# Additive attention scores: 16 tanh terms on three engines, or three groups of them as ratios of two matmuls

## The chip, the cores and the metric

The kernel runs on one core of one Trainium2 chip. TensorE (PE) multiplies matrices into PSUM, ScalarE (ACT) evaluates functions, VectorE (DVE) and GpSimd (POOL) work elementwise, SyncE (SP) and the queues of the other engines issue DMAs. The metric is the device time of one execution in microseconds (us). Before the change it was 9234.1 us, the median of 3 runs (9233.7 to 9238.85).

## The reference

The input x is (4, 32, 128, 128) in float32. Layer 0 (spectral convolutions with attention over 32 images) is not changed and is left out here. Layer 1 sees each of the 4 batch items as 4096 tokens of 128 channels:

```
h = layer norm of t
f = h @ W1[:128]                      # 16 numbers per token, as a query
g = h @ W1[128:]                      # 16 numbers per token, as a key
scores[i, j] = sum over a of w2[a] * tanh(f[i, a] + g[j, a] + b1[a])  + b2
e = exp(scores), for keys j before query i only (strictly)
t = t + (e @ h) / (sum of e + 1e-10)
t = t + two best of eight experts on layer norm of t, weighted by a softmax router
```

So for each pair of a query and an earlier key 16 tanh values are weighted and summed; that is some 33 million pairs.

## The kernel before, in words

`layer0` (L67 to L510) runs first and writes x1 to DRAM. Of it only a few rows are spoken of below: image norms with squares on ACT (L236), copies from PSUM by ACT and DVE in turn (L216, L218), the mix of modes with matmuls of 32 rows on different quadrants of the partitions (L453) and their products on DVE (L454), products and sums on POOL (L377, L489, L505), and powers on POOL (L64).

`layer1` (L513 to L804) goes through 16 chunks, 4 of each batch item, of IC = 1024 queries. Keys and queries are the same tokens, so a chunk also adds 8 blocks of 128 keys. In one chunk:

- `prepare` (called by `begin`) loads the tokens xc, norms them on DVE and POOL (`layer_norm`, L567 to L578, with the square at L572), transposes them on PE (L586), and makes the keys' numbers gk.
- `queries` makes, for each of the 16 hidden units, a tile f with the query's number on every partition (matmul L616, copy on DVE L623).
- For each block jb of 128 keys up to the diagonal there is one score tile of 128 keys by up to 1024 queries (only the columns from lo on). Each of the 16 units costs one tanh on ACT (L740), with the key's number as bias. For 5 units (A_PE) PE multiplies by w2 on a diagonal and sums in PSUM (L745). For the other 11, DVE multiplies and adds (L750, L754), and PE adds the sum through an identity matrix (L763). Then comes Exp (L765), and on the diagonal a mask by POOL (L767).
- After every four key blocks (JG) PE makes the attention's output po from e and the normed keys (L786), and DVE adds it to att (L796, L798).
- `finish` of the chunk before is written between two such groups: division by the sum (L635), addition to xc on POOL (L636), norm, transposes, router logits (L652), the two best experts in small DVE operations (L654 to L687), and then for each of 8 token blocks and both halves of the experts a matmul with 128 rows (L693), one with 1 row for the bias (L696), and four DVE operations that add the weighted result to xc (L698). The store follows. `begin` of the next chunk is written at the end of a chunk.

The order of the instructions on each engine is set by a scheduler of the tile framework from the program's order and the buffers of the pools. Each tag of a pool has its own buffers: 2 in PSUM for each of sc, m and o, 4 for th, 5 for e, 17 for f. An instruction waits on its own engine's queue, in order, until its operands are there and its buffer is free.

Of the kernel before, what the change touches and what calls it, by code (L numbers as in the profile page):

```python
# [7 lines left out]
F32 = mybir.dt.float32  # L8
# [5 lines left out]
P = 128  # L14
B, T, H, C = 4, 32, 128, 128  # x; an image of layer 0 is H x C, a block of layer 1 has H tokens
NH = 32  # heads of layer 0
KX, KY = 64, 33  # modes kept of a 128 x 128 image: rows 0..31, -32..-1; columns 0..32
KA = 17  # columns of the K, Q and V weights' modes (their rows: 0..15, -16..-1)
GI = 8  # images at a time
NPIX = H * C  # L20
A = 16  # width of layer 1's additive attention
A_PE = 5  # terms of its scores that the tensor engine sums; the vector engine sums the others
NE = 8  # experts
IC = 1024  # queries at a time
NB = IC // P
JG = 4  # key blocks for each accumulation of the attention's output

# places in the packed row of small parameters
# [5 lines left out]
def _constants():  # L34
    """Transforms and masks, from shapes alone."""
# [22 lines left out]

def _inv_std(nc, small, out, var, eps, nhalf):
    """out = (var + eps) ** -0.5"""  # L60
    n = out.shape[1]
    ve = small.tile([P, n], F32, name="ve", tag=f"ve{n}")
    nc.vector.tensor_scalar(ve, var, eps, None, ALU.add)  # L63
    nc.gpsimd.tensor_tensor(out, ve, nhalf.to_broadcast([P, n]), ALU.pow)  # L64


def layer0(tc, x, kcw, qcw, vcw, pcw, m0cw, m1cw, heads, small_row, by_p, inv_cols, x1):  # L67
# [9 lines left out]
    # (re | im) of a row transform of a real image, of i times it, and of minus it  # L77
# [20 lines left out]
    # score weights by mode, for the modes' real and imaginary parts  # L98
# [3 lines left out]
    # value weights: on partition 32g + head, columns ky = 4k + g  # L102
# [8 lines left out]
    with tc.tile_pool(name="l0_prep", bufs=1) as prep:  # L111

        def padded(src, name):
# [3 lines left out]
            for ri in range(2):  # L117
# [4 lines left out]
                # column 0 of a real image's spectrum is Hermitian  # L122
# [16 lines left out]
        # W = q conj(k), scaled for the inner product of two 64 x 64 images  # L139
# [27 lines left out]
        # row -32 of column 0 is its own mirror in a 64 x 64 image, and so real  # L167
# [11 lines left out]
        # G = P (v skip + V) + (P skip) V  # L179
# [32 lines left out]
    def evacuate(out, in_):  # L212
        """PSUM to SBUF, by the scalar and the vector engine in turn."""
        flip[0] ^= 1
        if flip[0]:
            nc.scalar.copy(out, in_)  # L216
        else:
            nc.vector.tensor_copy(out, in_)  # L218

    def image_means(src):  # L220
        """Means over each image of src [w, images, c], on every partition, in PSUM."""
        n = src.shape[1]
        s = small.tile([P, n], F32, name="s", tag=f"s{n}")
        nc.vector.tensor_reduce(s, src, AX.X, ALU.add)  # L224
        m = ps.tile([P, n], F32, name="m", tag="stat")
        nc.tensor.matmul(m, mean_w, s, start=True, stop=True)  # L226
        return m

    def inorm(src, out, w=None, b=None):
        """Instance norm of src [w, images, c] into out."""  # L230
# [15 lines left out]
    def transform(images, mirrored=None):  # L246
        """Modes X and iX of GI images [w, c], in PSUM, on partitions (part, kx) by (image, ky);
        mirrored gets column 32 of their 64 x 64 part."""
# [23 lines left out]
    def inverse(spec, take):  # L272
        """Images [w, c] of GI half spectra [(part, kx), image, ky]: take(k, four) gets those of
        images k .. k + 3, in PSUM."""
# [16 lines left out]
    for b in range(B):  # L291
# [60 lines left out]
        # column 32 of a 64 x 64 image is its own mirror, and its row -32 real  # L352
# [160 lines left out]
def layer1(tc, x1, w1, expert_w, expert_b, router_w, small_row, out):  # L513
    nc = tc.nc
    nblk = T  # blocks of 128 tokens of one b
# [3 lines left out]
        tc.tile_pool(name="l1_f", bufs=17),  # L519
        tc.tile_pool(name="l1_work", bufs=2),  # L520
        tc.tile_pool(name="l1_small", bufs=3),
        tc.tile_pool(name="l1_ps", bufs=2, space=PSUM),
    ]
    const, keys, fpool, work, small, ps = (p.__enter__() for p in pools)

    ident = const.tile([P, P], F32, name="ident1")
# [5 lines left out]
    w1t = const.tile([P, 2, A], F32, name="w1t")  # L532
    nc.sync.dma_start(out=w1t, in_=w1.rearrange("(s h) a -> h s a", s=2))
# [8 lines left out]
    # w2[a] on the diagonal  # L542
    w2d = const.tile([P, A_PE, P], F32, name="w2d")
    for a in range(A_PE):
        nc.vector.tensor_scalar(w2d[:, a], ident, par[:, W2 + a : W2 + a + 1], None, ALU.mult)
    # keys before queries: 1 where the column (query) is greater than the row (key)
# [11 lines left out]
    # ranks that fall with the expert's index, for ties  # L558
# [3 lines left out]

    def layer_norm(src, dst):
        """Layer norm over c of src [token, blocks, c] into dst."""
# [15 lines left out]
    def transposed(src):  # L580
        """[c, tokens] of src [token, blocks, c]."""
        xt = work.tile([P, IC], F32, name="xt", tag="xt")
        for k in range(0, NB, 4):
            pt = ps.tile([P, 4, P], F32, name="pt", tag="m")
            for j in range(4):
                nc.tensor.transpose(pt[:, j], src[:, k + j, :], ident)  # L586
            nc.vector.tensor_copy(xt[:, k * P : (k + 4) * P], pt.rearrange("p j t -> p (j t)"))
        return xt

    def prepare(b, i0, kx, gk):  # L590
        """Queries i0 .. i0 + IC: their tokens, and what they are as keys."""
# [3 lines left out]
        xt = transposed(kx[:, i0 : i0 + NB, 0:C])  # L595
        pg = ps.tile([P, NB, A], F32, name="pg", tag="m")
        for k in range(NB):
            nc.tensor.matmul(
                pg[:, k], xt[:, k * P : (k + 1) * P], w1t[:, 1], start=True, stop=True
            )  # L600
        nc.vector.tensor_tensor(
            gk[:, i0 : i0 + NB],
            pg,
            par[:, B1 : B1 + A].unsqueeze(1).to_broadcast([P, NB, A]),
            ALU.add,
        )
        return xc, xt

    def queries(xt):
        """Each query's part of the scores' argument, on every partition."""  # L610
        fq = []
        for a in range(A):
            f = fpool.tile([P, IC], F32, name="f", tag="f")
            for h in range(0, IC, 512):
                pf = ps.tile([P, 512], F32, name="pf", tag="m")
                nc.tensor.matmul(  # L616
                    pf,
                    w1t[:, 0, a : a + 1].to_broadcast([P, P]),
                    xt[:, h : h + 512],
                    start=True,  # L620
                    stop=True,
                )
                nc.vector.tensor_copy(f[:, h : h + 512], pf)  # L623
            fq.append(f)

        return fq

    def finish(b, i0, xc, att):
        """Adds the attention and the experts' layer to tokens xc, and stores them."""
# [9 lines left out]
        x2 = work.tile(full, F32, name="x2", tag="x2", bufs=1)  # L639
        layer_norm(xc, x2)  # L640
        x2t = transposed(x2)
# [8 lines left out]
        pl = ps.tile(fe, F32, name="pl", tag="m")  # L650
# [39 lines left out]
        for k in range(NB):  # L690
            for e0 in range(0, NE, 4):
                px = ps.tile([P, 4, C], F32, name="px", tag="m")
                nc.tensor.matmul(  # L693
                    px, x2t[:, k * P : (k + 1) * P], we[:, e0 : e0 + 4], start=True, stop=False
                )
                nc.tensor.matmul(px, ones1, eb[:, e0 : e0 + 4], start=False, stop=True)  # L696
                for e in range(4):
                    nc.vector.scalar_tensor_tensor(  # L698
                        xc[:, k],
                        px[:, e],  # L700
# [7 lines left out]
    def begin(b, i0, last):  # L708
        """As prepare, with the keys' tiles of the chunk before in the same b."""
        if i0 == 0:  # L710
            # normed tokens with a column of ones, and each key's part of the scores' argument
            kx = keys.tile([P, nblk, C + 1], F32, name=f"kx_{b}", tag="kx")
            nc.gpsimd.memset(kx[:, :, C : C + 1], 1.0)
            gk = keys.tile([P, nblk, A], F32, name=f"gk_{b}", tag="gk")
        else:
            kx, gk = last
        return (kx, gk, *prepare(b, i0, kx, gk))

    pending = None
    chunks = [(b, i0) for b in range(B) for i0 in range(0, nblk, NB)]  # L720
    ready = None
    for n_chunk, (b, i0) in enumerate(chunks):
        if ready is None:
            ready = begin(b, i0, None)
        kx, gk, xc, xt = ready
        fq = queries(xt)
        att = work.tile([P, NB, C + 1], F32, name="att", tag="att")
        group = []
        for jb in range(i0 + NB):
            lo = max(0, jb - i0) * P  # L730
            cuts = [(max(lo, h), h + 512) for h in range(0, IC, 512) if lo < h + 512]
# [129 lines left out]
```

## Time and profile before

| what | us |
| --- | --- |
| median of 3 runs | 9234.1 |
| span of the profiled execution | 9233.0 |
| first DMA issue of layer 1 (load of par) | 3061.0 |
| first normed keys ready | 3083.2 |
| start of the last finish | 9143.5 |
| busy PE, DVE, ACT, POOL | 6954.0, 6341.1, 5327.9, 625.2 |
| mean granted clock of PE | 0.795 of full |

The span runs from the first to the last instruction of the profiled execution. Busy times are sums over the whole span; the slices of the page, 40 equal ones of 231 us, tell where they fall. In a group's line the number after the bar is the busy time in us, then the mean of one instruction in ns, then the idle time ahead of it and what ended it. "PEld" is the loading of the stationary matrix, which can lie beside a matmul. A float32 matmul on PE appears as two records.

### The profile page before, as it was taken

The page shows a single profiled execution, that of the slowest core. Times are in us where ns is not written, and L with a number is a line of the kernel's source. Part 1 is how long each engine was busy: PE and PEld are TensorE (multiplying, and loading weights), DVE is VectorE, ACT ScalarE, POOL GpSimd, SP SyncE. Part 2 cuts the span into 40 slices and gives each one's busy share as a digit, 9 for nine tenths or more (in the row PEclk, how much of TensorE's full clock was granted, in tenths as well). Part 3 has the DMA queues.
Part 4 walks back from the last instruction along what each step waited for, and adds up shares of the span by engine and source line. Part 5 has one row for each costly group of instructions (what it writes and reads, how often), then busy time and mean ns, then how long its engine had stood idle before and what let it go on. Part 6 is the DMA issues. An engine that isn't in the chain of part 4 may idle for free.

```text
span 9233.0 us, 58632 instructions
## 1 busy us (share of the span) xinstructions
PE 6954.0 (75%) x19444; PEld 3500.2 (38%) x19444; DVE 6341.1 (69%) x8087; ACT 5327.9 (58%) x5917; POOL 625.2 (7%) x444
## 2 busy tenths in 40 slices
PE   3854954764584688787788878788888878887877
PEld 2443343343343333333333333343333333334333
DVE  4834754564474677777777777777877777777775
ACT  1012011011101477979867888986887895879795
POOL 1011111101101000000000000000000001000000
PEclk8655655655655789898999898898989899989987
DMA  1000000000000000000000000000000000000000
GB/s 29 2 5 14 2 3 16 2 3 5 4 0 7 12 5 5 0 5 0 0 5 5 5 0 5 0 0 10 0 5 0 5 0 5 5 3 0 3 0 3
DMA packets 72207, 42.00 MB, mean 5 GB/s; under 512 B 2524, under 2 KB 71262, under 8 KB 71871
## 3 DMA queue, kind: packets, MB, share of 16 engines
q1 hardware_dynamic: 45341, 24.55, 1.0%
q10 hardware_dynamic: 26562, 13.71, 0.5%
q8 instruction: 153, 2.51, 0.1%
q14 instruction: 151, 1.24, 0.0%
HBM read 18.82 MB, written 16.78 MB: 4 GB/s over the span
## 4 chain that ended last, share of the span: by engine, by line
PE 35%; ACT 34%; issue 13%; DVE 12%; POOL 5%; DMA 0%; SPq 0%; POOLq 0%; ACTq 0%; DVEq 0%
ACT th L740 29%; PE sc L745 13%; PE px L693 3%; PE px L696 3%; ACT e L765 3%; DVE s L224 2%; POOL r L64 2%; PE po L786 2%; PE sc L763 2%; PE pz L258 2%; DVE acc L754 2%; PE four L288 2%; PE sc L381 1%; DVE f L623 1%; PE pf L616 1%
## 5 line engine op out<-in xcount | busy, mean ns | idle before, releaser
L740 ACT ACTIVATE th<-f,gk 128x1024 f32<-128x1024 f32 (+7 forms) x5120 | 4676.1, 992 | 1087.0 <-PE sc L745 395.1
L754 DVE SCALAR_TENSOR_TENSOR acc<-th,par,acc 128x1024 f32<-128x1024 f32 (+7 forms) x3200 | 3512.8, 1098 | 832.9 <-ACT th L740 670.9
L745 PE MATMUL sc<-th,w2d 128*128 128x512 f32 (+3 forms) x5760 | 2866.5, 645 | 469.7 <-ACT th L740 450.2
L745 PEld LDWEIGHTS sc<-th,w2d 128*128 128x128 f32 x5760 | 1168.1, 217 | 1986.0 <-issue 1015.2
L786 PE MATMUL po<-kx,e 128*128 128x129 f32 x4224 | 609.7, 292 | 413.1 <-ACT e L765 316.6
L786 PEld LDWEIGHTS po<-kx,e 128*128 128x128 f32 x4224 | 526.0, 197 | 697.6 <-ACT e L765 503.4
L616 PE MATMUL pf<-xt,w1t 128*128 128x512 f32 x1024 | 527.8, 634 | 117.4 <-DVE f L623 115.7
L226 PE MATMUL m<-s,mean_w 128*128 128x8 f32 x384 | 112.5, 366 | 633.9 <-DVE s L224 626.5
L216 ACT COPY v<-pv 128x264 f32<-128x264 f32 x48 | 18.4, 384 | 986.7 <-PE pv L278 986.7
L698 DVE SCALAR_TENSOR_TENSOR xc<-px,wgt,xc 128x128 f32<-128x128 f32 x1024 | 340.4, 348 | 248.0 <-PE px L696 235.2
L763 PE MATMUL sc<-acc,ident 128*128 128x512 f32 (+3 forms) x1152 | 508.5, 559 | 0.0
L767 POOL TENSOR_TENSOR e<-e,later 128x128 f32<-128x128 f32 x128 | 88.5, 692 | 5313.5 <-ACT e L765 5313.5
L453 PE MATMUL mp<-pr,g_im 32*128 32x512 f32 x528 | 408.2, 1039 | 0.0
L453 PE MATMUL mp<-pr,g_re 32*128 32x512 f32 x528 | 403.9, 1067 | 2.9 <-DVE mix L454 2.9
L623 DVE COPY f<-pf 128x512 f32<-128x512 f32 x512 | 338.9, 684 | 51.9 <-PE pf L616 50.2
L226 PEld LDWEIGHTS m<-s,mean_w 128*128 128x128 f32 x384 | 96.5, 312 | 664.7 <-DVE s L224 418.6
L64 POOL TENSOR_TENSOR r<-ve,nhalf 128x8 f32<-128x8 f32 x128 | 210.1, 1641 | 2037.3 <-DVE ve L63 1967.3
L765 ACT ACTIVATE e<-sc,par 128x1024 f32<-128x1024 f32 (+3 forms) x320 | 306.3, 957 | 58.0 <-PE sc L763 52.0
L750 DVE TENSOR_SCALAR acc<-th,par 128x1024 f32<-128x1024 f32 (+3 forms) x320 | 210.8, 659 | 177.8 <-ACT th L740 177.8
L693 PE MATMUL px<-we,xt 128*128 128x512 f32 x512 | 331.8, 735 | 0.0
L616 PEld LDWEIGHTS pf<-xt,w1t 128*128 128x128 f32 x1024 | 174.5, 194 | 392.9 <-DVE f L623 338.8
L460 DVE TENSOR_REDUCE yf<-mix 128x16 f32<-128x1024 f32 x264 | 322.4, 1221 | 0.3
(230 smaller groups left out, 5777.8 us busy)
## 6 DMA issues: line engine op xcount, KB each, us to landing
x<-x SPq DMA_DIRECT2D x16, 512.0 KB, 3.2
xc<-x SPq DMA_DIRECT2D x16, 512.0 KB, 4.0
out<-xc ACTq DMA_DIRECT2D x16, 512.0 KB, 3.2
x<-in_x SPq DMA_DIRECT2D x8, 512.0 KB, 8.4
x<-in_x ACTq DMA_DIRECT2D x8, 512.0 KB, 9.2
pr<-pr SPq DMA_DIRECT2D x8, 128.0 KB, 2.9
pw<-in_pcw SPq DMA_DIRECT2D x1, 528.0 KB, 5.2
pr<-pr ACTq DMA_DIRECT2D x4, 128.0 KB, 2.3
```

The lines of the kernel that those rows point to most:

```text
L64: nc.gpsimd.tensor_tensor(out, ve, nhalf.to_broadcast([P, n]), ALU.pow)
L453: nc.tensor.matmul(mp, gw[pq, k, :], pr[pq, th], start=True, stop=True)
L616: nc.tensor.matmul(pf, w1t[:, 0, a : a + 1].to_broadcast([P, P]), xt[:, h : h + 512], start=True, stop=True,)
L623: nc.vector.tensor_copy(f[:, h : h + 512], pf)
L693: nc.tensor.matmul(px, x2t[:, k * P : (k + 1) * P], we[:, e0 : e0 + 4], start=True, stop=False)
L698: nc.vector.scalar_tensor_tensor(xc[:, k], px[:, e], wgt[:, k, e0 + e : e0 + e + 1], xc[:, k], ALU.mult, ALU.add,)
L740: nc.scalar.activation(th[:, lo:], fq[a][:, lo:], AF.Tanh, bias=gk[:, jb, a : a + 1])
L745: nc.tensor.matmul(sc[:, c0:c1], w2d[:, a], th[:, c0:c1], start=n_pe == 0, stop=False)
L754: nc.vector.scalar_tensor_tensor(acc[:, lo:], th[:, lo:], par[:, W2 + a : W2 + a + 1], acc[:, lo:], ALU.mult, ALU.add,)
L763: nc.tensor.matmul(sc[:, c0:c1], ident, acc[:, c0:c1], start=False, stop=True)
L765: nc.scalar.activation(e[:, lo:], sc[:, lo:], AF.Exp, bias=par[:, B2 : B2 + 1])
L786: nc.tensor.matmul(po[:, k - k0], t[:, k * P : (k + 1) * P], kx[:, j, :], start=j == js[0][0], stop=j == js[-1][0],)
```

## The change

The sum of w2[a] * tanh(u[a]) over a group of m units is written as a ratio. With tanh(u) = (e^u - e^-u) / (e^u + e^-u), the common denominator of m units is the product of the (e^u[a] + e^-u[a]), which is the sum over all 2^m choices of signs s of exp(sum of s[a] u[a]). The numerator is the same sum with each term multiplied by the sum of s[a] w2[a]. As u[a] is a key's part plus a query's part, each exponential is a key's factor times a query's factor, so both sums are inner products over the choices of signs, which are matmuls. Groups of 6, 5 and 5 units give 64, 32 and 32 choices, 128 rows in all.

- New inputs: the matrix of signs (17 x 128), W1 transposed, and a 17 x 2 array with b1, w2 and b2. At the start of layer 1 two matmuls make mq and mk (channels to sign choices) and a third kbias and kmul.
- `prepare` makes km = Exp(mk x + kbias), kc = km * kmul and qm = Exp(mq x). `queries` and the w2d diagonals are gone. km and kc are kept for all keys of a batch item.
- A chunk is done in two halves of QC = 512 queries. In each half `scores` is called for each key block: three matmuls D into three PSUM banks, Ln on ACT and Exp of its negative (1/D), three matmuls N, a product on DVE, two additions on POOL, Exp on ACT, and the mask on the diagonal on POOL.
- The attention's output is accumulated in PSUM over all key blocks of a half, and copied once to att.
- PSUM tags are now d (3 banks), n (3 banks) and o (2 banks), each with one buffer. The transposes, router logits and expert products use d and n as well: px takes the two in turn, one for each block of tokens.
- `finish` and `begin` are called behind key block 2 of the first and the second half.
- One table of functions that holds both Ln and Exp is loaded at the start of layer 1.

The core of the diff (comments that the change removes and the wiring of inputs are left out):

```diff
-IC = 1024  # queries at a time
+GROUP_SIZES = (6, 5, 5)
+DSCALE = 128.0
+IC = 1024
+QC = 512
+QB = QC // P
...
+def _signs():
+    s = np.zeros((A + 1, P), np.float32)
+    a = col = 0
+    for m in GROUP_SIZES:
+        for n in range(2**m):
+            for i in range(m):
+                s[a + i, col + n] = -1.0 if n >> i & 1 else 1.0
+        a, col = a + m, col + 2**m
+    s[A, : 2 ** GROUP_SIZES[0]] = 1.0
+    return s
...
-        tc.tile_pool(name="l1_ps", bufs=2, space=PSUM),
+        tc.tile_pool(name="l1_ps", bufs=1, space=PSUM),
...
+    tc.keep_in_program_order(nc.scalar.preload_act_table_set("natural_log_exp_and_others"))
...
+    def wide(name, tag):
+        return ps.tile([P, 3, 512], F32, name=name, tag=tag)
...
+        xt = transposed(kx[:, i0 : i0 + NB, 0:C], "d")
+        i = slice(i0 * P, i0 * P + IC)
+        for m, dst, bias, tag in ((mk, km[:, i], kbias, "n"), (mq, qm, 0.0, "d")):
+            pz = wide("pz", tag)
+            for h in range(2):
+                nc.tensor.matmul(
+                    pz[:, h], m, xt[:, h * 512 : (h + 1) * 512], start=True, stop=True
+                )
+            nc.scalar.activation(
+                dst.rearrange("p (h t) -> p h t", h=2), pz[:, :2], AF.Exp, bias=bias
+            )
+        nc.vector.tensor_scalar(kc[:, i], km[:, i], kmul, None, ALU.mult)
...
         for k in range(NB):
+            px = wide("px", "dn"[k % 2])
             for e0 in range(0, NE, 4):
-                px = ps.tile([P, 4, C], F32, name="px", tag="m")
+                pe = px[:, e0 // 4].rearrange("p (e c) -> p e c", e=4)
...
+    GROUPS = ((0, 64), (64, 96), (96, 128))
+    def scores(qm, q0, jb, own):
+        _, km, kc = own
+        lo = max(0, jb * P - q0)
+        j = slice(jb * P, (jb + 1) * P)
+        d = wide("d", "d")
+        for g, (r0, r1) in enumerate(GROUPS):
+            nc.tensor.matmul(
+                d[:, g, lo:], km[r0:r1, j], qm[r0:r1, lo:QC], start=True, stop=True
+            )
+        r = work.tile([P, 3, QC], F32, name="r", tag="r", bufs=3)
+        nc.scalar.activation(r[:, :, lo:], d[:, :, lo:], AF.Ln, scale=1.0 / DSCALE)
+        nc.scalar.activation(r[:, :, lo:], r[:, :, lo:], AF.Exp, scale=-1.0)
+        n = wide("n", "n")
+        for g, (r0, r1) in enumerate(GROUPS):
+            nc.tensor.matmul(
+                n[:, g, lo:], kc[r0:r1, j], qm[r0:r1, lo:QC], start=True, stop=True
+            )
+        nc.vector.tensor_tensor(r[:, :, lo:], n[:, :, lo:], r[:, :, lo:], ALU.mult)
+        e = work.tile([P, QC], F32, name="e", tag="e", bufs=4)
+        nc.gpsimd.tensor_tensor(e[:, lo:], r[:, 0, lo:], r[:, 1, lo:], ALU.add)
+        nc.gpsimd.tensor_tensor(e[:, lo:], e[:, lo:], r[:, 2, lo:], ALU.add)
+        nc.scalar.activation(e[:, lo:], e[:, lo:], AF.Exp)
+        if jb * P >= q0:
+            nc.gpsimd.tensor_tensor(e[:, lo : lo + P], e[:, lo : lo + P], later, ALU.mult)
+        return e
...
+        for half in range(2):
+            qb = i0 + half * QB
+            po = ps.tile([P, 2, 512], F32, name="po", tag="o")
+            for jb in range(qb + QB):
+                e = scores(qm[:, half * QC : (half + 1) * QC], qb * P, jb, own)
+                for k in range(QB):
+                    if jb > qb + k:
+                        continue
+                    nc.tensor.matmul(
+                        po[:, k // 2, (k % 2) * (C + 1) : (k % 2 + 1) * (C + 1)],
+                        e[:, k * P : (k + 1) * P],
+                        own[0][:, jb, :],
+                        start=jb == 0 and k % 2 == 0,
+                        stop=jb == qb + k,
+                        skip_group_check=True,
                     )
+                if jb == 2 and half == 0 and pending is not None:
+                    finish(*pending)
+                    pending = None
+                if jb == 2 and half == 1 and n_chunk + 1 < len(chunks):
+                    ready = begin(*chunks[n_chunk + 1], own)
+            nc.vector.tensor_copy(
+                att[:, half * QB : (half + 1) * QB].rearrange("p (h k) c -> p h (k c)", h=2),
+                po[:, :, : 2 * (C + 1)],
+            )
```

In the changed kernel's own numbering the D matmuls are L736, Ln L740, Exp of its negative L741, the N matmuls L744, the product L747, the two additions L749 and L750, the Exp of the scores L751, the mask L753, the output matmuls L780, the copy to att L793, and the experts' matmuls L711 and L714.

## The prediction

> **What bounds the kernel now.** I read the page first (its totals, slices and the chain that ended last), then the groups by line and shape, then the stretches, then single rows of the timeline.
>
> ```profile
> span 9233.0 us, 58632 instructions
> ...
> PE 6954.0 (75%) x19444; PEld 3500.2 (38%) x19444; DVE 6341.1 (69%) x8087; ACT 5327.9 (58%) x5917; POOL 625.2 (7%) x444
> ...
> PEclk8655655655655789898999898898989899989987
> ...
> PE 35%; ACT 34%; issue 13%; DVE 12%; POOL 5%; DMA 0%; SPq 0%; POOLq 0%; ACTq 0%; DVEq 0%
> ACT th L740 29%; PE sc L745 13%; PE px L693 3%; PE px L696 3%; ACT e L765 3%; DVE s L224 2%; POOL r L64 2%; PE po L786 2%; PE sc L763 2%; PE pz L258 2%; DVE acc L754 2%; PE four L288 2%; PE sc L381 1%; DVE f L623 1%; PE pf L616 1%
> ...
> L740 ACT ACTIVATE th<-f,gk 128x1024 f32<-128x1024 f32 (+7 forms) x5120 | 4676.1, 992 | 1087.0 <-PE sc L745 395.1
> L754 DVE SCALAR_TENSOR_TENSOR acc<-th,par,acc 128x1024 f32<-128x1024 f32 (+7 forms) x3200 | 3512.8, 1098 | 832.9 <-ACT th L740 670.9
> ```
>
> See that layer 0 (first 33% of the span; its slices have ACT at 0 to 2 tenths) is untouched, and that behind it ACT is nearly full with 5120 tanh. PE and DVE keep pace with ACT, so layer 1 runs near ACT's throughput. The span is 9233.0 and the median of the runs 9234.1, so 1 us lies outside; I sum against the span and add it.
>
> **What goes.** 4676.1 us of tanh on ACT (L740), 3512.8 + 210.8 on DVE (L754, L750), 2866.5 + 508.5 on PE (L745, L763), and the query copies (527.8 PE at L616, 338.9 DVE at L623). The bound goes with them; what is late next is the new step.
>
> **What comes: one step for 512 queries and 128 keys.** There are 144 such steps in each b, 576 in all; those on the diagonal are 512, 384, 256, 128 wide, so they equal 528 full ones. In each, three D matmuls, ACT Ln and Exp over 1536 columns, three N matmuls, a DVE product of 1536, two POOL sums of 512, ACT Exp of 512, four output matmuls. No row of before has these; their prices come from these rows (mean ns is the number before the second bar):
>
> ```profile
> L454 DVE TENSOR_TENSOR mix<-mp,xf 128x512 f32<-128x512 f32 x264 | 182.4, 691 | 0.0
> L216 ACT COPY it<-pi 128x512 f32<-128x512 f32 x96 | 56.4, 587 | 72.5 <-PE pi L253 72.5
> L236 ACT ACTIVATE sq<-an 128x1024 f32<-128x1024 f32 x48 | 50.7, 1057 | 256.7 <-DVE an L234 256.7
> ...
> L636 POOL TENSOR_TENSOR xc<-xc,att 128x1024 f32<-128x1024 f32 x16 | 34.8, 2172 | 73.4 <-DVE att L635 73.4
> L489 POOL TENSOR_TENSOR spec<-spec,im 128x264 f32<-128x264 f32 x32 | 23.7, 740 | 435.3 <-DVE im L486 435.3
> ```
>
> - ACT: tanh takes 397 ns at 128 columns and 1142 at 1024, so 0.83 ns a column; L236 leaves 208 fixed from SBUF, L216 163 from PSUM. Exp of 1536: 1.48 us; Ln of 1536: 1.44; Exp of 512: 0.63.
> - DVE product: L454 and L635 (1024 columns, 1216 ns) give 1.04 ns a column and 0.157 fixed: 1.757 us.
> - POOL sum: L636 and L489 give 1.89 ns a column, with the 128x128 mask (454 ns at best) 1.92 and 0.209 fixed: 1.19 us. L377 (1909 for 1024, same engine and form) gives 1.06 as lower end, L505 (2344) 1.26 as upper; beside a busy DVE a L572 row went from 1.89 to 2.81, which would be 1.4 or so. I take 1.19, the nearest forms.
> - Hand-overs: ACT to DVE 0.04, DVE to POOL 0.08, POOL to ACT 0.04 taken as POOL to DVE's; POOL to POOL 0.1, unseen, between 0 and 0.2.
>
> **What bounds the step: the order on ACT.** The changed kernel's static order on ACT is Ln(j+1), E(j), Exp(j+1), Ln(j+2), where E is the Exp of 512. So Exp(j+1) stands behind E(j), which waits for both POOL sums, which wait for the product, which waits for Exp(j). Nothing of step j+1 but its Ln and its matmuls passes this ring: T = 1.48 + 0.04 + 1.757 + 0.08 + 1.19 + 0.1 + 1.19 + 0.04 + 0.63 - 0.1 (the next ACT start stands about 0.1 ahead of a modelled end) = 6.41 us. ACT's own work is only 3.44. By columns it is 5.26 + 1.15 fixed: 528 x 5.26 + 576 x 1.15 = 3440 us. POOL's ends move T to 6.1 and 6.9: -170 and +260 us.
>
> **PE in the step.** L693's 256 calls leave 512 records: an fp32 matmul is two passes. Single records of 512 columns start 0.43 us apart at full clock, 0.853 at half. D and N have 64, 32 and 32 rows. One after another they would be 3 x 0.86 each at full clock, 3 x 1.71 at half; beside one another 0.86 and 1.71. In layer 0 matmuls of different 32-row groups do run beside one another:
>
> ```profile
> 288.15 1.13 PE L453 MATMUL mp<-pr,g_re 32*128 32x512 f32 x4
> ...
> 289.01 1.20 PE L453 MATMUL mp<-pr,g_im 32*128 32x512 f32 x4
> ```
>
> By their records nine passes begin between 287.72 and 289.62, 1.9 us; in a row their eight distances of 0.43 would need 3.4. No row has 64 rows beside 32. Lower end: full overlap, D 1.75 and N 1.75 at half clock, outputs (8 passes of 0.215) 1.95: 5.4 us, under T even cold, so PE costs nothing. Upper end: no overlap, 12 us cold. I take overlap, the nearest row. A change of tile size does cost: from L693 (128 rows) to L696 (1 row) the next pass starts 0.09 us later than the usual pitch and its weight load shows; cold, four passes take 4.0 instead of 3.4, so 0.2 to 0.3 a change.
>
> [...]
>
> **The rest of layer 1.** (a) Layer 0 and the first chunk's norm end as now (first normed keys at 3083.2); transposes, Exps: first score at about 3101. (b) At each of 32 half ends Ln of the next half stands behind the last E: 1.35, together 43. (c) 15 begins, in the order between steps with the tags of d and n: two Exps of 1024, transposes, copies: about 10 each, 150 (between 0 and 25). (d) 15 finishes. In before the scheduler lets the experts run beside scores. In the changed order, the 64 expert passes stand in one row on PE ahead of the next D, and their PSUM tiles take d's and n's only buffers, so no score runs beside them. Their price is the last finish of before, which is bare:
>
> ```profile
> 9168.00:9233.00 65.00, 58.80 (x59) 14.48 (x58) 22.45 (x64) 0.00 (x0) 0.00 (x0) 0.50 0.03 8
> ```
>
> (length, busy PE, weight loads, DVE, ACT, POOL, granted clock 0.50.) From x2 (9157.3) to the last expert pass (9226.8) it is 69.5 us, PE-bound: 16 x 4.0 at half clock. With a refill and the norm's rows slipped in between the products of three steps, 78 each: 1170. (e) The last finish, as now: 91 (9143 to 9233).
>
> The clock: in this trace it is 1.0 or 0.5 for each 3.41 us. Weighting PE's records by rows used, it stays 1.0 above about 0.36 of a window and comes back only above some 0.77. A finish begins with idle PE, so I price it cold.
>
> **Sum:** 3101 + 3440 + 43 + 150 + 1170 + 91 = 7995, with the 1 us outside some **8000 us**, -13%.
>
> **Rivals.**
> 1. *Slower: the array drains between 64 and 32 rows, at half clock.* D and N are two blocks each, 1.71 + 1.71 with two or three changes: 4.2; with outputs 1.95, T = 10.4, PE-bound. PE's weighted work is 5.2 of 10.4, 0.50, under the 0.77 that brings the clock back, so it stays cold. As columns and fixed: 528 x 8.55 + 576 x 1.9 = 5610 in place of 3440: **10,160 us**. It decides from T > 6.41 + (9233 - 7995) / 528 = 8.75 us, which needs both the drain and the low clock: drained but warm, PE needs 5.5, under the ring's 6.41. For it: no row with mixed sizes, every finish leaves a cold clock. Against: the L453 rows; overlapped, even cold, the weighted share would be 5.2 / 6.41 = 0.81 and bring the clock back.
> 2. *No overlap at all, cold:* T = 12.0, some 10,900. L453 speaks against it.
> 3. *Drained, the clock now high, now low:* T between 6.4 and 10.4, 8400 to 9900.
> 4. *Experts at full clock or beside scores:* 32 instead of 64 us, 16 times: 7490. The PE order speaks against it.
> 5. *ACT's throughput bounds:* T about 3.5, 1.9 ms: 6450. Needs Exp(j+1) ahead of E(j); the static order says no.
> 6. *It doesn't do what it says: Ln and Exp reload tables.* Two loads a step of 1.283 (the one load row) would add 1478: 9470. The static order has one load in layer 1, ahead of all; excluded.
>
> **How the numbers follow.** Forecast 7600 to 8400: 0.47. Rival 4: 0.08. Rival 5: 0.03. Rival 3: 0.08, half of it on the faster side. Rival 1: 0.27. Rival 2: 0.07. Faster by over 0.2% (what a measurement here can tell from no change): 0.47 + 0.08 + 0.03 + 0.04 = 0.62, less 0.02 for within 0.2%; slower 0.38. The likeliest's own range is 7600 to 8400. For 8 in 10 it must reach rival 1 with some margin and most of rival 4: 7450 to 10,300.
>
> **What would show it.** Right: Ln to Ln of 6.1 to 6.9 us in mid-half; ACT's Exp of 1536 released by E or idle on POOL ahead of E; ACT near 55% busy in steps, POOL some 40%; PE idle; D's three matmuls starting within 0.1 us; bare stretches of 65 to 80 us, 15 of them, with L711 and L714 on PE at clock 0.5. Wrong: D's second matmul starting 0.9 or 1.7 us after the first; PE busy over 90% at clock 0.5; POOL sums over 1.4; table loads; scores beside experts.

## The result, and the profile after

The changed kernel takes 9772.3 us (median of 4 runs, 9772.0 to 9780.9) against 9234.8 before: a ratio of 1.0586, 95% interval 1.0571 to 1.0601. It is slower by 5.9%. The prediction on record was 8000 us, faster; the time lies in the stated range only because that range was drawn to reach its first rival, which had a chance of 0.27.

The page of the changed kernel, its totals, clock and chain:

```profile
span 9770.3 us, 47522 instructions
...
PE 8433.3 (86%) x18298; PEld 3629.0 (37%) x18298; DVE 3283.9 (34%) x4406; ACT 2234.9 (23%) x2237; POOL 1950.6 (20%) x1596
...
PEclk9555655655655555555555555555555555555555
...
PE 76%; issue 10%; DVE 8%; POOL 4%; ACT 2%; DMA 0%; SPq 0%; POOLq 0%; DVEq 0%; ACTq 0%
PE d L736 22%; PE n L744 22%; PE po L780 11%; PE px L711 5%; PE px L714 5%; DVE s L240 2%; PE pz L274 2%; POOL r L80 2%; PE four L304 1%; PE sc L397 1%; POOL pb L393 1%; PE pi L269 1%; PE pt L299 1%; ACT sq L252 1%; PE m L242 1%
```

ACT fell from 5327.9 to 2234.9 us and DVE from 6341.1 to 3283.9, as the change promises. PE rose from 6954.0 to 8433.3, and the chain that ended last, which ran 35% over PE and 34% over ACT, now runs 76% over PE. The clock row, 8 and 9 behind layer 0 before, is 5 to the end.

The groups of the step, by shape (busy us, mean ns of one, then idle time ahead and its releaser). In a matmul's row `64*128` is a stationary matrix of 64 rows and 128 columns; its rows lie on 64 of the 128 partitions, and which ones is its row group:

```profile
L736 PE MATMUL d<-qm,km 32*128 32x512 f32 x1920 | 1040.8, 1121 | 0.0
L744 PE MATMUL n<-qm,kc 32*128 32x512 f32 x1920 | 1006.4, 1124 | 0.0
L736 PE MATMUL d<-qm,km 64*128 64x512 f32 x960 | 979.3, 1121 | 4.7 <-ACT r L740 3.5 <-ACT qm L639 1.1
...
L747 DVE TENSOR_TENSOR r<-n,r 128x1536 f32<-128x1536 f32 x480 | 843.7, 1758 | 3476.4 <-PE n L744 3361.1 <-ACT r L741 115.3
...
L740 ACT ACTIVATE r<-d 128x1536 f32<-128x1536 f32 x480 | 695.9, 1450 | 3611.7 <-PE d L736 3611.7
L750 POOL TENSOR_TENSOR e<-e,r 128x512 f32<-128x512 f32 x480 | 620.6, 1293 | 37.5
```

DVE's product and ACT's Ln have nearly the durations that were predicted (1.758 and 1.450 us), but both wait thousands of us for PE, and PE's own groups wait for almost nothing. One step from the timeline (start, length, engine, line):

```profile
6002.34 2.09 PE L780 MATMUL po<-kx,e 128*128 128x129 f32 x8
...
6004.36 4.08 PE L736 MATMUL d<-qm,km 64*128 64x512 f32 x6
...
6006.36 0.50 PEld L736 LDWEIGHTS d<-qm,km 32*128 32x128 f32 x4 [1.50 <-issue]
...
6008.36 4.08 PE L744 MATMUL n<-qm,kc 64*128 64x512 f32 x6
6008.48 1.45 ACT L740 ACTIVATE r<-d 128x1536 f32<-128x1536 f32 x1 [6.70 <-PE d L736]
...
6012.37 2.09 PE L780 MATMUL po<-kx,e 128*128 128x129 f32 x8
```

Output, D, N, output: PE has no gap, and the step is 10.03 us (6002.34 to 6012.37), D and N 4.01 each. The weights of the 32-row matmuls are loaded 2.00 us after D's begin. The single records say the same: D's two passes (records) of 64 rows start at 6004.357 and 6005.372; then, 0.99 us after the second, the two matmuls of 32 rows start together, at 6006.360 and 6006.366, and their second passes at 6007.373 and 6007.380. So here 32 runs beside 32, and neither beside 64.

The stretch of layer 1 up to the last finish (length, busy PE, weight loads, DVE, ACT, POOL, clock):

```profile
3100.00:9680.00 6580.00, 6494.45 (x12676) 2457.28 (x12672) 1585.04 (x2219) 1835.19 (x1769) 1558.38 (x1354) 0.51 0.01 3
```

PE is busy 99% of it, at half clock for nearly all of it. The clock did come back: in this stretch it is full 21 times, for 3.4 to 10.2 us each, 164 us in all. One of these, from 6065.50 to 6075.74, is filled first by matmuls of 128 rows (a begin and an output) and then by D and N:

```profile
6071.78 2.17 PE L744 MATMUL n<-qm,kc 64*128 64x512 f32 x4
...
6072.83 0.29 PEld L744 LDWEIGHTS n<-qm,kc 32*128 32x128 f32 x2 [0.76 <-issue]
6073.88 2.40 PE L736 MATMUL d<-qm,km 64*128 64x512 f32 x6
```

At full clock the 64-row matmul of N and one of its 32-row matmuls (the other stands behind D here) are still two blocks, of 1.05 us each (6071.78 to 6072.83 to 6073.88). Four such blocks are 4.2 us, and the output matmuls take 1.0 at full clock (e1, 6000.214 to 6001.210): an estimate of 5.2 us a step for a PE that stays at full clock. But the full clock is lost each time: in all 21 cases its last window of 3.41 us has PE work of only 0.28 to 0.37, weighted by rows (the last section says how).

The theory from here is the prediction's first rival: (1) the tiles of 64 and of 32 rows do not run side by side, so D and N are two blocks each, 2.00 us a block above; (2) what PE runs weighs too little to bring the clock back (the prediction's 5.2 us of full-row work at half clock in 10.03, 0.52, where it read some 0.77 from the trace of before) or to keep it (the 0.28 to 0.37 of the 21 cases); so PE bounds. The rivals to it: that only the clock, only the overlap, or the order on ACT is to blame.

### The profile page after: what moved, and what is told of

It is laid out like the page before. It is cut to its first block, busy times and chain, and to the rows that moved or that the text cites. A ratio compares the mean times of both kernels' runs of the same rounds, so it can differ in the third digit from the quotient of the medians.

```text
span 9770.3 us, 47522 instructions
## 1 busy us (share of the span) xinstructions
PE 8433.3 (86%) x18298; PEld 3629.0 (37%) x18298; DVE 3283.9 (34%) x4406; ACT 2234.9 (23%) x2237; POOL 1950.6 (20%) x1596
## 4 chain that ended last, share of the span: by engine, by line
PE 76%; issue 10%; DVE 8%; POOL 4%; ACT 2%; DMA 0%; SPq 0%; POOLq 0%; DVEq 0%; ACTq 0%
PE d L736 22%; PE n L744 22%; PE po L780 11%; PE px L711 5%; PE px L714 5%; DVE s L240 2%; PE pz L274 2%; POOL r L80 2%; PE four L304 1%; PE sc L397 1%; POOL pb L393 1%; PE pi L269 1%; PE pt L299 1%; ACT sq L252 1%; PE m L242 1%
## 5 line engine op out<-in xcount | busy, mean ns | idle before, releaser
L747 DVE TENSOR_TENSOR r<-n,r 128x1536 f32<-128x1536 f32 (+1 forms) x576 | 935.6, 1624 | 3957.0 <-PE n L744 3841.7
L736 PE MATMUL d<-qm,km 32*128 32x512 f32 (+6 forms) x3456 | 2239.5, 1052 | 4.7 <-ACT r L740 3.5
L744 PE MATMUL n<-qm,kc 32*128 32x512 f32 (+6 forms) x3456 | 2179.9, 1054 | 1.1 <-DVE r L747 1.1
L740 ACT ACTIVATE r<-d 128x1536 f32<-128x1536 f32 (+1 forms) x576 | 773.7, 1343 | 4258.8 <-PE d L736 4258.8
L749 POOL TENSOR_TENSOR e<-r 128x512 f32<-128x512 f32 (+1 forms) x576 | 677.5, 1176 | 4638.7 <-DVE r L747 4553.6
L780 PEld LDWEIGHTS po<-kx,e 128*128 128x128 f32 x4224 | 936.3, 324 | 804.8 <-ACT r L741 576.2
L744 PEld LDWEIGHTS n<-qm,kc 32*128 32x128 f32 (+1 forms) x3456 | 575.7, 302 | 1523.3 <-issue 1463.3
L780 PE MATMUL po<-kx,e 128*128 128x129 f32 x4224 | 1101.7, 438 | 27.2 <-ACT e L751 17.3
L736 PEld LDWEIGHTS d<-qm,km 32*128 32x128 f32 (+1 forms) x3456 | 597.3, 303 | 1025.5 <-issue 891.2
L741 ACT ACTIVATE r<-r 128x1536 f32<-128x1536 f32 (+1 forms) x576 | 787.8, 1368 | 4.2
L750 POOL TENSOR_TENSOR e<-e,r 128x512 f32<-128x512 f32 (+1 forms) x576 | 690.1, 1198 | 45.1
L711 PE MATMUL px<-we,xt 128*128 128x512 f32 x512 | 530.0, 1140 | 31.7 <-DVE xc L716 31.7
L714 PE MATMUL px<-eb,ones 1*128 1x512 f32 x512 | 527.7, 1132 | 0.0
L751 ACT ACTIVATE e<-e 128x512 f32<-128x512 f32 (+1 forms) x576 | 337.7, 586 | 351.5 <-POOL e L750 351.5
L711 PEld LDWEIGHTS px<-we,xt 128*128 128x128 f32 x512 | 129.5, 313 | 391.9 <-issue 313.7
```

Of the source, the lines that this page charges most:

```text
L711: nc.tensor.matmul(pe, x2t[:, k * P : (k + 1) * P], we[:, e0 : e0 + 4], start=True, stop=False)
L714: nc.tensor.matmul(pe, ones1, eb[:, e0 : e0 + 4], start=False, stop=True)
L736: nc.tensor.matmul(d[:, g, lo:], km[r0:r1, j], qm[r0:r1, lo:QC], start=True, stop=True)
L740: nc.scalar.activation(r[:, :, lo:], d[:, :, lo:], AF.Ln, scale=1.0 / DSCALE)
L741: nc.scalar.activation(r[:, :, lo:], r[:, :, lo:], AF.Exp, scale=-1.0)
L744: nc.tensor.matmul(n[:, g, lo:], kc[r0:r1, j], qm[r0:r1, lo:QC], start=True, stop=True)
```

## The experiments

Times are of one execution beside one of the kernel before (9214.7 to 9226.2) unless a ratio is given. "Step" is the median distance from one Ln of 1536 columns to the next in the middle of a half (336 of them: from key block 4 on, up to the first block on the diagonal). "Ring" is the prediction's chain over ACT, DVE and POOL that the order on ACT makes.

**e1: all 128 rows in every matmul.** The queries' factors are kept in three copies, each zero outside its group's rows.

```diff
-    GROUPS = ((0, 64), (64, 96), (96, 128))
+    GROUPS = ((0, 128, 0), (0, 128, 1), (0, 128, 2))
...
-                d[:, g, lo:], km[r0:r1, j], qm[r0:r1, lo:QC], start=True, stop=True
+                d[:, g, lo:], km[r0:r1, j], qm[r0:r1, q, lo:QC], start=True, stop=True
```

> Each of the six matmuls of a step uses all 128 rows: the queries' factors are kept in three copies with zeros outside one group's rows. Nothing can overlap, so PE has more passes than in the changed kernel (12 of 512 columns in a row), but no change of tile size, and every busy moment counts with all rows. Theory (drain between 64 and 32 rows, and a clock that stays low because the weighted share of PE is too small): the clock comes back to 1.0, PE needs 12 x 0.43 + 0.88 = 6.0 us a step, the ring over ACT, DVE and POOL bounds with 6.4 to 6.7 us, total 7500 to 8000. Rival (the clock stays at half whatever the rows): 12 x 0.853 + 1.95 = 12.2 us a step, total some 10900.

Measured: 8272.8 us, step 6.57. From its timeline one D, the two Exps on ACT and the next D; then its stretch of layer 1 (columns as above):

```profile
6001.21 2.74 PE L749 MATMUL d<-qm,km 128*128 128x512 f32 x6
...
6006.10 0.63 ACT L764 ACTIVATE e<-e 128x512 f32<-128x512 f32 x1 [0.66 <-POOL e L763]
6006.63 1.47 ACT L754 ACTIVATE r<-r 128x1536 f32<-128x1536 f32 x1
...
6007.78 2.74 PE L749 MATMUL d<-qm,km 128*128 128x512 f32 x6
```

```profile
3100.00:8200.00 5100.00, 4579.09 (x12694) 2111.72 (x12695) 1592.62 (x2232) 1920.59 (x1801) 1565.33 (x1358) 0.87 0.01 3
```

With nothing side by side, D takes 2.58 us (six passes 0.43 apart) in place of 4.01, because the clock is back (0.87 in this stretch, 0.51 in the changed kernel's). The step is the ring: ACT's Exp of 1536 stands behind the Exp of the scores, and that waits for POOL. The total missed the expected 7500 to 8000; a finish still costs some 82 us here (e7).

**e2: three groups of 32 rows.** The sixteenth hidden unit is left out of the scores.

```diff
-GROUP_SIZES = (6, 5, 5)
+GROUP_SIZES = (5, 5, 5)
...
-    GROUPS = ((0, 64), (64, 96), (96, 128))
+    GROUPS = ((0, 32), (32, 64), (64, 96))
```

> Three groups of five units, 32 rows each, in three row groups; the sixteenth unit is left out of the scores. All tiles of D and N have one size. Theory (64 beside 32 rows does not overlap, equal tiles do): the three matmuls of D start within some 20 ns of one another, D and N take 2.0 us each at half clock, PE 6.0, the ring bounds with 6.4 to 6.7 us a step, total 7900 to 8100, with the clock still at half (weighted share 0.66). Rival (at most two matmuls run beside one another, whatever their size): D and N stay at 4.0, a step at 10.0, total 9770.

Measured: 8257.4 us, above the expected 7900 to 8100; step 6.56. A D and the two Exps from its timeline, and the stretch of layer 1:

```profile
6000.68 2.08 PE L736 MATMUL d<-qm,km 32*128 32x512 f32 x6
...
6004.54 0.63 ACT L751 ACTIVATE e<-e 128x512 f32<-128x512 f32 x1 [0.27 <-POOL e L750]
6005.07 1.47 ACT L741 ACTIVATE r<-r 128x1536 f32<-128x1536 f32 x1
```

```profile
3100.00:8200.00 5100.00, 4265.56 (x12711) 1941.12 (x12710) 1600.76 (x2267) 1884.33 (x1770) 1560.38 (x1357) 0.55 0.01 3
```

Six passes within 2.0 us, the three matmuls starting at 6000.675, 6000.682 and 6000.689, with the clock at 0.55. Overlap alone takes PE off the path here, at half clock (busy 4266 of 5100 us). e1 and e2 together: in this kernel matmuls of 128 rows at a clock of 0.87 suffice, and so does full overlap at 0.55. Both end at the same ring, with the Exp of the scores waiting for POOL; the changed kernel has neither.

**e3: 64 rows in all of D and N.** The groups of 32 are computed on rows 64 to 127, with zeros in the other's half.

```diff
-    GROUPS = ((0, 64), (64, 96), (96, 128))
+    GROUPS = ((0, 64, 0), (64, 128, 0), (64, 128, 1))
```

> The two groups of 32 are each computed with 64 rows (rows 64 to 127, zeros in the other group's half of the queries' factors), so all three matmuls have 64 rows: the first on rows 0 to 63, the others on 64 to 127. Theory: the first and the second run beside one another, the third beside the next first where the order lets it; at half clock PE needs 7 to 9 us a step with a weighted share of 0.75 to 0.77, at the edge of what brings the clock back; total 9000 to 9400 at half clock, some 7950 if the clock comes back, bounded by the ring. Rival (the row group of the first, not its size, keeps the others out): six matmuls in a row, 12 us a step, total some 10900 at half clock.

Measured: 8344.2 us, between the two expected totals; step 6.57 (mean 6.82), clock 0.79 in layer 1. The row group of the 64-row matmul is not what kept the others out: here one of D and one of N run beside one another, both of 64 rows, both started at 6000.15:

```profile
6000.15 1.06 PE L749 MATMUL d<-qm,km 64*128 64x512 f32 x1
6000.15 0.33 PEld L749 LDWEIGHTS d<-qm,km 64*128 64x128 f32 x1 [0.51 <-issue]
6000.15 1.06 PE L757 MATMUL n<-qm,kc 64*128 64x512 f32 x1
```

The clock goes up and down, and was high more often than the first of the expected totals (9000 to 9400) had it.

**e4: only the order on ACT.** The changed kernel, with the Exp of the scores of step j behind the Exp of 1536 of step j+1.

```diff
+        ee = nc.scalar.activation(e[:, lo:], e[:, lo:], AF.Exp)
+        if after is not None:
+            tc.add_manual_dep(ee.ins, after.ins.name, ...)
```

> The changed kernel with its matmuls as they are; only the order on ACT differs: the Exp of the scores of step j is issued behind the Exp of 1536 columns of step j+1, so that the ring through POOL no longer passes a whole step. Theory (PE at half clock with two blocks for each of D and N bounds the step): no effect, 10.0 us a step, total 9680 to 9790. Rival (the ring on ACT, DVE and POOL has a part in the 10 us): a step falls below 9.5, total under 9500.

Measured: 9899.9 us, step 10.03 as in the changed kernel. The scheduler also moved the output matmuls to between the 64-row and the 32-row matmuls of N; PE has no gap there either. The ring has no part in the changed kernel's step. The total is 128 us over the changed kernel's and above what was expected. As the step is equal, this lies at the two ends of the halves, most of which became 3 to 6 us longer (a bare half end went from 9.3 to 11.0); why, was not followed further.

**e5 and e6: that order with 128 and with 64 rows.** The edit of e4 on top of e1 and of e3.

> The kernel with 128 rows in every matmul and the new order on ACT. Theory (there the ring of 6.57 us bounds, of which PE's 6.0 to 6.1 at full clock is next): a step falls to 6.0 to 6.2, total 7950 to 8100. Rival (PE bounds there too, or POOL): 6.5 us a step, total 8250.

> The kernel with 64 rows in all of D and N and the new order on ACT. Theory: at full clock PE needs 4 blocks of 0.86, the outputs 0.88 and up to four changes of tile size of 0.2, some 5.0 us; the ring is out of the way, so a step takes 4.9 to 5.4 while the clock is high and 8 to 9 while it is low; total 7400 to 7900 if it is mostly high, 9000 and more if low. Rival (the ring still bounds): 6.57 and 8340.

Measured: 8155.4 and 8101.6 us. Both missed. In e5 the step alternates between 5.6 and 7.8 (median 5.64, mean 6.53): the scheduler, which still chose PE's order, put output matmuls between the matmuls of one N, and these wait for the Exp of the scores:

```profile
5977.81 1.02 PE L763 MATMUL n<-qm,kc 128*128 128x512 f32 x2
...
5979.87 1.16 PE L828 MATMUL po<-kx,e 128*128 128x129 f32 x8 [1.04 <-ACT e L770]
```

So the wait moved to PE. e6 is uneven too (mean 6.12, clock 0.80), and its PE rows were not followed.

**e7: the experts' bias without its 1-row matmuls.** On top of e1.

```diff
-                nc.tensor.matmul(pe, ones1, eb[:, e0 : e0 + 4], start=False, stop=True)
...
+                nc.tensor.transpose(pw[: NB * NE, 0, :P], wgt.rearrange("p k e -> p (k e)"), ident)
...
+                    nc.tensor.matmul(pv[:, h], wt, ebd[:, h * 4 : h * 4 + 4].rearrange("p k c -> p (k c)"), start=True, stop=True)
```

> The kernel with 128 rows, with the experts' bias no longer added by a matmul of one row and 512 columns for each of 16 products of a finish; instead the weights are transposed once and two matmuls of 64 rows make the weighted bias of all tokens. Theory (the finish is bound by PE at half clock, 64 passes of 1.0 us, and nothing runs beside it): 32 passes and the size changes go, the stretch of a finish falls from 89 us by 30 to 40, total 7630 to 7800. Rival (DVE's products or the router bound the finish): the total stays within 100 us of 8271.

Measured: 7701.4 us, as expected. From its first pass to its last the experts' row on PE takes 65.2 us in 14 of the 16 finishes of the changed kernel and of e1, and 31 to 36 here. Of the 571 us saved against e1, 16 x 33 = 528 lie in the finishes (the median step with a finish in it went from 89.1 to 55.9).

**e8: both sums on DVE.** On top of e7.

```diff
-        nc.gpsimd.tensor_tensor(e[:, lo:], r[:, 0, lo:], r[:, 1, lo:], ALU.add)
-        nc.gpsimd.tensor_tensor(e[:, lo:], e[:, lo:], r[:, 2, lo:], ALU.add)
+        nc.vector.tensor_tensor(e[:, lo:], r[:, 0, lo:], r[:, 1, lo:], ALU.add)
+        nc.vector.tensor_tensor(e[:, lo:], e[:, lo:], r[:, 2, lo:], ALU.add)
```

> The kernel with 128 rows and the weighted bias; both sums of a step move from POOL to DVE, and nothing else. Theory (ring of 6.57 us, of which the two POOL sums and their hand-overs are 2.7): DVE's sums take 0.69 each, the ring falls to 5.4, PE's 6.04 takes over, a step at 6.05 to 6.2, total 7400 to 7530. Rival (PE or ACT bounds at 6.57 already): 7700.

Measured: 7325.4 us, step 6.04, PE's own sum. The ring was real, and POOL's two sums (2.5 of its 6.57 us) were its longest part; the total is 75 us under the expected range.

**e9 to e11: 64 rows with the sums on DVE, then the order of PE and ACT fixed by hand, with 64 and with 128 rows.** e9 is e3 with the edits of e7 and e8, and e10 and e11 start from it. In them PE does D(j), N(j), output of step j-2; ACT does Ln(j), Exp(j), Exp of the scores of j-1. Every matmul of a step is queued behind the one traced before it:

```diff
+    def pe(ins):
+        order["pe"] = behind(ins, order["pe"])
...
-                nc.tensor.matmul(
+                pe(nc.tensor.matmul(
```

> As the run with the sums on DVE, but with 64 rows in all of D and N. Theory: the ring of 5.4 us bounds while the clock is high (PE about 5.0), 8 to 9 us a step while it is low; the weighted share at full clock is 3.46 of 5.4, 0.64, so it stays high once it is, and the finish, now of 128-row matmuls, can bring it back; total 7050 to 7500. Rival (the clock falls and stays low): 9000 and more.

> As the run before, with the order on PE and ACT fixed: D(j), N(j), output matmuls of step j-2 on PE; Ln(j), Exp(j), Exp of scores of step j-1 on ACT. The ring is gone. Theory: PE bounds with 4.5 to 5.0 us a step at full clock, total 6750 to 7200; at half clock 8.5 to 9. Rival (ACT or DVE holds the step at 5.4 all the same): no better than the run before.

> The same fixed order with 128 rows in every matmul. Theory: PE has no gap, 12 x 0.43 + 0.88 = 6.04 us a step at full clock, and as nothing else can bound it, total 7350 to 7450; half ends cost 1 us each. Rival (DVE or ACT bounds): the same as the run with the sums on DVE in its order, or slower.

Measured: 7090.0 us (step 5.28), 6754.4 (median 5.11, down to 4.72) and 7275.8 (6.04). The totals of e9 and e10 lie in their expected ranges, the median step of e10 a little over its 4.5 to 5.0, and e11 is 74 us under its range. e11 shows PE bare at full clock, 6.04; e10 is under that by 0.93 us, so 64-row tiles side by side did pay here, where the clock stayed high (0.93 in layer 1 in the next run). A step of e10 on PE:

```profile
5999.66 1.99 PE L790 MATMUL n<-qm,kc 64*128 64x512 f32 x6
...
6001.58 1.16 PE L853 MATMUL po<-kx,e 128*128 128x129 f32 x8
...
6002.57 1.76 DVE L794 TENSOR_TENSOR r<-n,r 128x1536 f32<-128x1536 f32 x1 [1.52 <-ACT r L786]
```

N's six passes take 1.9 us in place of 4.01, at full clock and with 64 rows beside 64.

**e12: e10 again, timed in rounds.** No edit.

> The kernel of the run with 64 rows and the fixed order again, now timed in rounds against the kernel before: 6750 to 6760 us, a ratio of 0.731 to 0.733.

Measured: 6762.4 us, ratio to the kernel before 0.7335, 95% interval 0.7323 to 0.7347; both stand just above the expected values. It is faster than both kernels and keeps the ratio form of the scores with all 16 units.

## Why the prediction was wrong

- **The step that failed:** "I take overlap, the nearest row." The L453 rows show tiles of one size on different row groups. They say nothing of 64 beside 32, which the prediction said itself; it took the row for more than it showed. D and N took 4.01 us each in place of 1.75, and e2 and e3 show that tiles of equal size overlap, of 32 rows and of 64. That "the array drains between 64 and 32 rows", as the first rival has it, no row of before showed. What the changed kernel's rows show is that the 32 rows start 0.99 us after the last 64-row pass has started (6005.372 to 6006.360), and not beside it; in these runs matmuls on different row groups ran at once only where their tiles had one size.
- **The clock followed from it.** The prediction made the clock's return depend on overlap (0.81 with it, 0.50 without). Without it the share is 5.2 of 10.03, 0.52, and the clock 0.51 in layer 1. In e1, where every pass of a step counts with 128 rows, the share of a step is 6.04 of 6.57, 0.92, and the clock 0.87, finishes included. Whether overlap of the same 128 rows would have kept the clock up was not run; e2 has 96 rows and stayed at 0.55.
- **The point of decision held.** The prediction said slower needs D and N in two blocks each and the low clock, both. e1 (no overlap, high clock) and e2 (overlap, low clock) are at 6.57 and 6.56 a step and at 0.90 of the time before. No run kept 64 beside 32 rows at full clock for long, but the blocks at 6071.78 price it at 5.2 us a step, near the prediction's 5.5 and under the ring.
- **The first rival's price:** 10,160 against 9772. Its steps and half ends were 5610 + 43 and took 5358; of these 295 us, 528 x 0.37 = 195 is the step of 10.4 that measured 10.03. Another 99 lie in the start, begins and finishes, by the sum below.
- **The ring was right.** T = 6.41 was predicted, 6.56 to 6.57 measured in e1 to e3. POOL's two sums take 1.26 and 1.27 to 1.29 where 1.19 was taken, the end of the range (L505's 1.26); that is 0.15 of the 0.16. The hand-over from POOL to POOL, put in as 0.1 and unseen before, is 0.08 (37.5 us of idle time ahead of 480 rows of L750). DVE's product came out as forecast, 1.758 for 1.757, in part by luck: the two rows named for it give 1.03 ns a column and 0.166 us fixed, which is 1.74.
- **The finishes were nearly right.** 78 us was predicted for each; a step with a finish takes 84.17 (the median of the 12 inside a batch item; the 3 that open one take 81.0), so 74.1 more than 10.03. Begins: 7.8 where 10 was taken.
- **The sum.** By term: fixed start 3094 (-7), finishes 15 x 74.1 (-58), begins 15 x 7.8 (-33), last finish 90 (9680.2 to 9770.3; -1, as 9143 to 9233 is 90 too). What is left of the span, 5358 us, is the steps with the half ends, where 3440 + 43 = 3483 was forecast (+1875). Together +1776 on 7995, 9771.
- The exclusions held: one table load in layer 1 (at 3058.9), no D or N between the experts' passes of any finish, no bound by ACT (busy 1835 us of the 6580 in layer 1).

## What to carry to other kernels

In these runs matmuls on different row groups ran side by side only when their tiles had one size (32 beside 32, 64 beside 64), so try padding a smaller group with zeros before mixing sizes: e1 and e3 gained 15% over the changed kernel by it. Count PE's work by rows when you ask whether the clock will be high: here 99% busy with 32 and 64 rows ran at 0.51, and e1's matmuls with 128 rows, most of them zeros, ran at 0.87 and were the faster ones (D in 2.58 us in place of 4.01). When a throughput bound goes, write down the static order on each engine and sum the ring that it makes; here it was 6.57 us where no engine but PE had more than 3.6 (ACT: 1.45 + 1.47 + 0.62).

## What the runs showed of the hardware that was not expected

- In the changed kernel a change of tile size costs some 0.3 us at half clock, half of it ahead of the first pass after the change and half on that pass (medians over layer 1, at half clock). D's first pass starts 0.352 us after the last output pass (332 times), where output passes follow one another in 0.214 (3520 times): +0.14. D's second 64-row pass follows the first in 1.015 (464 times), where passes of 512 columns that come without a change follow in 0.853 (6076.084 and 6076.937): +0.16. From 64 to 32 rows it is 0.988 (422 times), again +0.14. The kernel has four such changes for D and N: 8 x 0.853 + 4 x 0.3 = 8.0 us, the two blocks of 4.01. At full clock the same two parts are 0.09 (0.522 from 6071.257 to 6071.779) and 0.10 (0.534 from there to 6072.313), against a usual 0.43.
- PE at 6494 us busy of 6580 in layer 1 stayed at clock 0.51, so busy time is not what decides the clock here; work weighted by rows fits. The clock's records read 1.0 or 0.5, in stretches of 3.41 us or a multiple of it (544 of them in the trace of before, 124 in the changed kernel's). Count a pass of 512 columns as 0.43 us at full clock and 0.853 at half, times its rows / 128, in each window of 3.41 us in which the clock is one or the other. In the changed kernel at half clock, none of some 2170 windows with a share between 0.30 and 0.70 was followed by a full one, and all 54 above 0.80 were. At full clock, all 62 up to 0.38 were followed by half clock and all 124 from 0.40 on by full. Without the weight it does not fit: of the 1770 half-clock windows of layer 1 (3100 to 9680) with a share above 0.80, 18 were followed by a full one. The trace of before has it as the prediction read it: at half clock 1 of 855 windows below 0.74, 16 of 34 between 0.74 and 0.80 and all 255 above were followed by a full one, at full clock none of 260 up to 0.36 and all 1261 from 0.40 on.
